# The row of target scores in layer 0: transposed on VectorE in 32x32 blocks before it goes to scratch

## The chip, the cores and the metric

One Trainium2 chip, one core. The time is device microseconds of one execution. Beside the runs that are timed, one execution is taken with the hardware profiler; all rows shown here come from such executions. Engines: PE is TensorE (PEld its weight loads), DVE is VectorE, ACT is ScalarE, POOL is GpSimd, SP is SyncE, which here issues every DMA.

## What is computed

Four graph layers over 32 graphs of 512 nodes with 128 features; every layer is added to its input after a layer norm and a relu. Layers 1 to 3 are products with the adjacency matrix and small weights. The change lies in layer 0, which is a kind of graph attention:

```
x_h   = elu(h @ Wi + bi)                       # h = relu(layernorm(x)), [32, 512, 128]
a_src = x_h @ We[:H, 0]                        # one score per node
a_tgt = x_h @ We[H:, 0]                        # one score per node
e     = sigmoid(a_tgt[:, :, None] + a_src[:, None, :] + be[0])
e     = e * (adj + ALPHA * (1 - (adj != 0)))   # [32, 512, 512]
agg   = einsum('bij,bjh->bih', e, x_h)
self_part = x_h * sum(e, axis=-1)
out   = concat([elu(concat([agg, self_part]) @ Wn + bn), x_h]) @ Wm + bm
```

For e, the target score of every node i is needed along the free axis, on all 128 partitions, while the source score of node j is a value per partition. The scores come out of a matmul with the nodes on the partitions. So the targets have to be turned from columns into a row, and the row spread over the partitions.

## The kernel before

The kernel first lists all operations of all graphs with `op(engine, us, due, emit, reads, writes, ...)`, and then a planner (`Plan.order`) puts them into one fixed order for each engine. The planner keeps a clock of its own: `us` is the time that an operation holds its engine, `result` how much later its output is known, and `due` only ranks the operations that are ready on an engine at a moment. Buffers are slots of a kind: 36 of "f" (SBUF, 128x512), 8 of "s" (SBUF, small), 8 of "b" (PSUM), 4 of "d" (the row, in DRAM), 8 of "m" (DRAM), 6 of "x". An operation that takes a new slot is placed only when one is free on the planner's clock. Operations marked `two`, and all POOL operations, are kept apart in that plan. On the chip the order is fixed, and each instruction waits by semaphores for what it needs, in its engine's order[...]. The plan also exists a second time, for an adjacency matrix that is not exact in a short format; it isn't executed here.

Several graphs are under way at once: while layers 1 to 3 of one group of four graphs run, layer 0 of the next group is woven in between. Layer 1 takes five steps per graph; each ends with `turned` (L333): a transpose in blocks on VectorE (L337), a write to scratch "m" (L340) and a read back in another order (L342), 256 KB each. Then ScalarE rounds the state (L672), VectorE takes the rest (L675), and TensorE multiplies with the adjacency matrix (L686). L352 is the copy of a PSUM result to SBUF; L357 is any product with a 128x128 weight.

Layer 0 of graph b (`layer0`, L455): TensorE forms the messages and the two scores of each node (L469); VectorE scales the scores into the small tile `ends` (L476): columns 0 to 3 are source scores of the four chunks of 128 nodes, columns 4 to 7 the targets. For the first four graphs the targets are spread by TensorE (L493). For the other 28:

```
op("SP", 0.6, due + 10, gather, [ends], [row], result=11.0)
op("SP", 0.6, due + 14, lambda: nc.sync.dma_start(
    at(tgt), at(row).to_broadcast([P, N])), [row], [tgt], keep=KEEP, result=7.0)
```

`gather` (L488) writes the four columns into the 2 KB row "d" in DRAM, one element of 4 bytes at a time, and the read (L502) brings that row to each of the 128 partitions. Then four tanh operations on ScalarE, one for each chunk of source nodes, make e with the source score as bias (L507), VectorE multiplies by the mask (L510), GpSimd adds up (L516), TensorE aggregates (L525).

Of the kernel before, what the change touches and what calls it, by code (L numbers as in the profile page):

```python
# [13 lines left out]
AF = mybir.ActivationFunctionType  # L14
ALU = mybir.AluOpType

P = 128
# [21 lines left out]
class Plan:  # L39
# [13 lines left out]
    def op(self, eng, us, due, emit, reads=(), writes=(), two=False, keep=0, result=None):  # L53

        o = Op(eng, us, self.RESULT[eng] if result is None else result, emit, two, keep)
        for v in reads:
            o.before.add(v.writer)  # L60
        for v in writes:
            o.before.update(v.readers)
            if v.writer:
                o.before.add(v.writer)
            elif v.kind and v.slot is None:
                o.takes.append(v)
        for v in reads:
            v.readers.append(o)
        for v in writes:
            v.writer, v.readers = o, []  # L70
        o.vals = [v.whole or v for v in dict.fromkeys([*reads, *writes])]
        for v in o.vals:
            v.left += 1
        for v in [*reads, *writes, *o.vals]:
            self.vals[v] = True
        o.before -= {o, None}
        o.due = max([due, *(b.due for b in o.before)])
        for b in o.before:
            b.after.append(o)
        self.ops.append(o)  # L80
# [100 lines left out]
def tile_four_graph_layers(  # L181
# [27 lines left out]
    nc = tc.nc  # L209
    B, N, D = x.shape  # L210
    NC = N // P
    G = 4
# [10 lines left out]
    slots = {"x": 6, "f": 36, "q": 4, "s": 8, "d": 4, "m": 8, "b": 8}  # L223
    plan = Plan(slots, ahead=60.0, last=(B - 2) * PACE)
    op = plan.op
# [4 lines left out]
    dram = ctx.enter_context(tc.tile_pool(name="dram", bufs=1, space=bass.MemoryType.DRAM))  # L230

    def buffers(pool, kind, n, shape, dt=F32):
        return [pool.tile(shape, dt, tag=f"{kind}{i}", name=f"{kind}{i}") for i in range(n)]
# [3 lines left out]
        "f": buffers(pool, "f", slots["f"], [P, 512]),  # L237
        "q": buffers(pool, "q", slots["q"], [P, 512], F32R),
        "s": buffers(pool, "s", slots["s"], [P, 12 * NC]),
        "d": buffers(dram, "d", slots["d"], [1, N]),  # L240
        "m": buffers(dram, "m", slots["m"], [P, N]),
        "b": buffers(psum, "b", slots["b"], [P, 512]),
    }
# [1 line left out]
    def at(v):  # L245
        if v.tile is not None:
            return v.tile
        return places[v.kind][v.slot] if v.whole is None else at(v.whole)[:, v.part]
# [8 lines left out]
    def chunks(t):  # L257
        return t.rearrange("p (c d) -> p c d", c=NC)
# [65 lines left out]
    def transposed(src, due):  # L324

        pt = Val("b")
        def emit():
            for c in range(NC):
                nc.tensor.transpose(at(pt)[:, ts(c, P)], at(src)[:, ts(c, P)], at(ident))  # L329
        op("PE", T_TR, due, emit, [src, ident], [pt])  # L330
        return pt
# [18 lines left out]
    def copied(src, due, us=T_COPY):  # L350
        t = Val("f")
        op("ACT", us, due, lambda: nc.scalar.copy(at(t), at(src)), [src], [t])  # L352
        return t
# [58 lines left out]
    for jc in range(NC):  # L412
        pt, z, odd = Val("b"), Val("f"), Val("f")
        def turn(jc=jc, pt=pt):
            for ic in range(NC):
                nc.tensor.transpose(at(pt)[:, ts(ic, P)], at(A_nat[ic])[:, ts(jc, P)], at(ident))
# [38 lines left out]
    def layer0(b, h, due):  # L455
        KEEP = 12
        hT = copied(transposed(h, due), due)
        d = due + 6
        xhT = elu(product(Wi_sb, hT, d), bi_sb, bi_half, d, KEEP)

        d = due + 14
        msg, ends = Val("f"), Val("s")
        for half in range(2):
            pt = Val("b")
            def cut(pt):
                return at(pt)[:, : 2 * (P + 2)].rearrange("p (c d) -> p c d", c=2)
            def send(pt=pt, half=half):
                for c in range(2):
                    nc.tensor.matmul(  # L469
                        cut(pt)[:, c, :], at(xhT)[:, ts(2 * half + c, P)], at(W_tok),  # L470
                        start=True, stop=True,
                    )
            def take(pt=pt, half=half):
                nc.scalar.copy(chunks(at(msg))[:, ts(half, 2), :], cut(pt)[:, :, :P])
            def score(pt=pt, half=half):
                nc.vector.tensor_scalar(  # L476
                    at(ends)[:, : 2 * NC].rearrange("p (k c) -> p c k", k=2)[:, ts(half, 2), :],
                    cut(pt)[:, :, P:], 0.5, at(be_quarter), op0=ALU.mult, op1=ALU.add,
                )
            op("PE", 2 * T_NARROW, d, send, [xhT, W_tok], [pt])  # L480
            op("DVE", 0.14, d, score, [pt, be_quarter], [ends])
            op("ACT", 0.3, d, take, [pt], [msg])

        d = due + 20
        row, tgt = Val("d"), Val("f")
        def gather():
            with nc.allow_non_contiguous_dma(reason="a column of chunks becomes a row"):
                nc.sync.dma_start(  # L488
                    at(row).rearrange("o (c p) -> p (o c)", c=NC), at(ends)[:, NC : 2 * NC]
                )  # L490
        def spread():
            for c in range(NC):
                nc.tensor.transpose(  # L493
                    at(tgt)[:, ts(c, P)],
                    at(ends)[:, NC + c : NC + c + 1].to_broadcast([P, P]), at(ident),
                )
        if b < G:
            tgt = Val("b")
            op("PE", T_TR, d, spread, [ends, ident], [tgt])
        else:  # L500
            op("SP", 0.6, due + 10, gather, [ends], [row], result=11.0)
            op("SP", 0.6, due + 14, lambda: nc.sync.dma_start(  # L502
                at(tgt), at(row).to_broadcast([P, N])), [row], [tgt], keep=KEEP, result=7.0)
        es = []
        for jc in range(NC):
            e = Val("f")
            op("ACT", T_ACT, d, lambda e=e, jc=jc: nc.scalar.activation(  # L507
                at(e), at(tgt), AF.Tanh, bias=at(ends)[:, jc : jc + 1]), [tgt, ends], [e],
                keep=KEEP if jc == 0 else 0)
            op("DVE", T_VEC, d + jc, lambda e=e, jc=jc: nc.vector.scalar_tensor_tensor(  # L510
                at(e), at(e), 1.0, at(mask)[:, jc, :], op0=ALU.add, op1=ALU.mult),
                [e, mask], [e], two=True)
            es.append(e)
        sums = [Val("f"), Val("f")]
        def add(dst, a, c):
            op("POOL", 1.4, d, lambda: nc.gpsimd.tensor_tensor(  # L516
                at(dst), at(a), at(c), op=ALU.add), [a, c], [dst])
        add(sums[0], es[0], es[1])
        add(sums[1], es[2], es[3])
        add(sums[0], sums[0], sums[1])  # L520

        d = due + 30
        pn = Val("b")
        for jc in range(NC):
            op("PE", T_MM, d, lambda jc=jc: nc.tensor.matmul(  # L525
                at(pn), at(msg)[:, ts(jc, P)], at(es[jc]), start=jc == 0, stop=False),
                [msg, es[jc]], [pn])

        if b < G:
            ps = product(ones, sums[0], d)  # L530
        else:
            high, low, ps = Val("q"), Val("q"), Val("b")
            op("ACT", T_COPY, d, lambda: nc.scalar.copy(at(high), at(sums[0])), [sums[0]], [high])
            op("DVE", T_VEC, d, lambda: nc.vector.tensor_tensor(
                at(low), at(sums[0]), at(high).bitcast(F32), op=ALU.subtract),
                [sums[0], high], [low], two=True)
            def total():
                for n, part in enumerate((low, high)):
                    nc.tensor.matmul(at(ps), at(ones_r), at(part), start=n == 0, stop=n == 1)
            op("PE", 2 * T_PASS, d, total, [high, low, ones_r], [ps])  # L540
        own = Val("f")
        op("DVE", T_VEC, d, lambda: nc.vector.tensor_tensor(
            at(own), at(xhT), at(ps), op=ALU.mult), [xhT, ps], [own])
        product(Wn_sb, own, d, pn, start=False)
        recv = elu(pn, bn_sb, bn_half, d + 6, 2, ALPHA / 2)

        d = due + 44
        po = Val("b")
        def emit():
            for c in range(NC):  # L550
                for n, src in enumerate((recv, xhT)):
                    nc.tensor.matmul(  # L552
                        at(po)[:, ts(c, P)], at(src)[:, ts(c, P)], at(Wm_sb)[:, n, :],
                        start=n == 0, stop=n == 1,
                    )
        op("PE", 8 * T_NARROW, d, emit, [recv, xhT, Wm_sb], [po])
        add_to_x(b, po, d)
# [294 lines left out]
```

## Time and profile before

| | before |
|---|---|
| median of 3 runs | 1746.38 us (1745.01 to 1746.55) |
| profiled execution, its own time | 1748.12 us |
| its span in the profile | 1746.3 us |
| PE busy | 1695.5 us, 97% |
| DVE busy | 1479.3 us, 85% |
| ACT busy | 1135.2 us, 65% |
| POOL busy | 399.8 us, 23% |
| moved by DMA | 112.07 MB, mean 64 GB/s |

A row of the table of groups names the line, the engine, the operation and the tiles (out<-in, with buffer numbers left out), then the shapes, how often it ran, its busy time in us and the mean ns of one, and behind the second bar the idle time of the engine just before these instructions with what ended it. In a timeline, each row has its start in us, its duration, and in brackets the idle time of the engine before it and the releaser. In the list of DMA issues the last number is the median time in us from issue to landing. In a list of waits the three numbers are the us in total, how often, and the longest. PE's ends are modelled, so its busy time is somewhat too large.

### The profile page before, as it was taken

The page shows a single profiled execution, that of the slowest core. Times are in us where ns is not written, and L with a number is a line of the kernel's source. Part 1 is how long each engine was busy: PE and PEld are TensorE (multiplying, and loading weights), DVE is VectorE, ACT ScalarE, POOL GpSimd, SP SyncE. Part 2 cuts the span into 40 slices and gives each one's busy share as a digit, 9 for nine tenths or more (in the row PEclk, how much of TensorE's full clock was granted, in tenths as well). Part 3 has the DMA queues.
Part 4 walks back from the last instruction along what each step waited for, and adds up shares of the span by engine and source line. Part 5 has one row for each costly group of instructions (what it writes and reads, how often), then busy time and mean ns, then how long its engine had stood idle before and what let it go on. Part 6 is the DMA issues. An engine that isn't in the chain of part 4 may idle for free.

```text
span 1746.3 us, 21006 instructions
## 1 busy us (share of the span) xinstructions
PE 1695.5 (97%) x6829; PEld 1098.0 (63%) x6829; DVE 1479.3 (85%) x3213; ACT 1135.2 (65%) x2155; POOL 399.8 (23%) x312
## 2 busy tenths in 40 slices
PE   5899999999999999999999999999999999999998
PEld 3555555566666666665666666666666656656797
DVE  6899999999898887888888898888899879878752
ACT  6767765778666666665765667666768656655451
POOL 4521210332222211222212221122232212001110
PEclk9999999999999999999999999999999999999999
DMA  4022322322222222223221221222322131221201
GB/s 109 7 53 75 85 73 73 81 52 85 52 58 61 79 67 46 74 75 55 67 55 60 79 61 61 67 52 81 67 67 55 50 84 61 73 72 58 76 13 48
DMA packets 164534, 112.07 MB, mean 64 GB/s; under 512 B 23232, under 2 KB 139840, under 8 KB 164416
## 3 DMA queue, kind: packets, MB, share of 16 engines
q1 hardware_dynamic: 164416, 110.65, 23.9%
q8 instruction: 55, 0.90, 0.3%
q14 instruction: 63, 0.52, 0.2%
HBM read 60.23 MB, written 50.39 MB: 63 GB/s over the span
## 4 chain that ended last, share of the span: by engine, by line
PE 76%; DVE 13%; DMA 4%; ACT 3%; issue 2%; SPq 0%; DVEq 0%; ACTq 0%
PE b L357 33%; PE b L686 17%; PE b L769 9%; PE b L760 6%; DMA f<-m 4%; PE b L525 4%; PE b L552 3%; DVE f L510 2%; PE b L329 2%; DVE f L704 2%; PE b L743 2%; PE b L469 1%; DVE f L337 1%; DVE f L723 1%; DVE r L675 1%
## 5 line engine op out<-in xcount | busy, mean ns | idle before, releaser
L686 PE MATMUL b<-A_r,r 128*128 128x512 f32 x1536 | 427.6, 421 | 4.3 <-DVE r L675 4.2
L352 ACT COPY f<-b 128x512 f32<-128x512 f32 x448 | 256.5, 588 | 210.6 <-PE b L686 119.2
L686 PEld LDWEIGHTS b<-A_r,r 128*128 128x128 f32 x1536 | 287.2, 189 | 109.6 <-issue 38.9
L391 POOL TENSOR_TENSOR s<-s,nhalf 128x4 f32<-128x4 f32 x128 | 156.2, 1221 | 735.9 <-DVE s L389 707.8
L769 PE MATMUL b<-r,A_r 128*128 128x512 f32 x768 | 306.3, 499 | 0.0
L704 DVE TENSOR_TENSOR f<-f,b 128x512 f32<-128x512 f32 x320 | 213.6, 679 | 56.5 <-PE b L357 54.0
L399 ACT ACTIVATE f<-x,s 128x128 f32<-128x128 f32 x512 | 209.9, 488 | 22.3 <-DVE s L394 22.2
L769 PEld LDWEIGHTS b<-r,A_r 128*128 128x128 f32 x768 | 140.6, 189 | 102.6 <-issue 91.5
L516 POOL TENSOR_TENSOR f<-f,f 128x512 f32<-128x512 f32 x96 | 154.1, 1608 | 207.4 <-DVE f L510 131.1
L362 ACT ACTIVATE f<-f,b4w 128x512 f32<-128x512 f32 x160 | 115.8, 724 | 127.3 <-DVE f L704 126.6
L337 DVE STREAM_TRANSPOSE f<-f 128x512 f32<-128x512 f32 x160 | 176.5, 1105 | 0.3
L675 DVE TENSOR_TENSOR r<-f,r 128x512 fp32r<-128x512 f32 x192 | 141.3, 739 | 37.1 <-ACT r L672 37.0
L357 PE MATMUL b<-f,u5T 128*128 128x512 f32 x320 | 163.2, 595 | 8.7 <-DVE f L711 8.7
L357 PE MATMUL b<-f,w4T 128*128 128x512 f32 x320 | 165.2, 599 | 4.1 <-ACT f L352 4.0
L357 PE MATMUL b<-f,w3T 128*128 128x512 f32 x320 | 163.8, 594 | 0.0
L357 PE MATMUL b<-f,w5T 128*128 128x512 f32 x320 | 163.2, 595 | 0.0
L357 PE MATMUL b<-f,u3T 128*128 128x512 f32 x320 | 162.7, 592 | 0.0
L721 DVE TENSOR_TENSOR f<-f,f 128x512 f32<-128x512 f32 x160 | 121.5, 761 | 39.3 <-ACT f L362 39.1
L760 PEld LDWEIGHTS b<-V,f 128*128 128x128 f32 x1024 | 131.7, 191 | 31.1 <-issue 25.1
L362 ACT ACTIVATE f<-b,b5w 128x512 f32<-128x512 f32 x160 | 109.7, 688 | 60.4 <-PE b L357 60.2
L362 ACT ACTIVATE f<-f,b3w 128x512 f32<-128x512 f32 x160 | 115.0, 721 | 50.8 <-DVE f L704 50.5
L525 PE MATMUL b<-f,f 128*128 128x512 f32 x256 | 130.9, 596 | 3.2 <-issue 3.0
(95 smaller groups left out, 2489.9 us busy)
## 6 DMA issues: line engine op xcount, KB each, us to landing
m<-f SPq DMA_DIRECT2D x160, 256.0 KB, 2.0
f<-m SPq DMA_DIRECT2D x160, 256.0 KB, 2.8
x<-in_x_dram SPq DMA_DIRECT2D x32, 256.0 KB, 4.5
out_dram<-x SPq DMA_DIRECT2D x32, 256.0 KB, 2.4
f<-d SPq DMA_DIRECT2D x28, 256.0 KB, 4.1
f<-in_adj_dram SPq DMA_DIRECT2D x4, 256.0 KB, 4.6
f<-in_L_gnn_weight_dram SPq DMA_DIRECT2D x2, 224.0 KB, 2.6
d<-s SPq DMA_DIRECT2D x28, 2.0 KB, 9.1
```

The lines of the kernel that those rows point to most:

```text
L337: op("DVE", 1.03, due, lambda: nc.vector.transpose(at(blocks).rearrange("p (q c f) -> p q c f", c=NC, f=32), at(src).rearrange("p (c i q) ...
L352: op("ACT", us, due, lambda: nc.scalar.copy(at(t), at(src)), [src], [t])
L357: op("PE", T_MM, due, lambda: nc.tensor.matmul(at(dst), at(w), at(src), start=start, stop=stop), [src, w], [dst])
L362: op("ACT", us, due, lambda: nc.scalar.activation(at(dst), at(src), AF.Tanh, bias=at(bias), scale=scale), [src, bias], [dst])
L391: op("POOL", 1.2, due, lambda: nc.gpsimd.tensor_tensor(stat(SCALE), stat(VAR), at(neg_half), op=ALU.pow), [s, neg_half], [s])
L399: nc.scalar.activation(at(h)[:, ts(c, P)], at(X[b])[:, c, :], AF.Relu, bias=stat(SHIFT)[:, c : c + 1], scale=stat(SCALE)[:, c : c + 1],)
L525: op("PE", T_MM, d, lambda jc=jc: nc.tensor.matmul(at(pn), at(msg)[:, ts(jc, P)], at(es[jc]), start=jc == 0, stop=False), [msg, es[jc]], [pn])
L675: op("DVE", T_VEC, due, lambda: nc.vector.tensor_tensor(part(lo), whole(), part(hi).bitcast(F32), op=ALU.subtract), [src, hi], [lo], two=two)
L686: nc.tensor.matmul(at(pa), at(part)[:, ts(jc, P)], at(adjT)[:, jc, :], start=jc == n == 0, stop=jc == NC - 1 and n == PARTS - 1,)
L704: op("DVE", T_VEC, d, lambda: nc.vector.tensor_tensor(at(s), at(u), at(pg), op=ALU.add), [u, pg], [s])
L760: nc.tensor.matmul(at(pz)[:, ts(i, D)], at(hT[i])[:, ts(ic, P)], at(V[k]), start=i == 0, stop=last and i == G - 1,)
L769: nc.tensor.matmul(at(pz), at(adjT)[:, jc, ts(ic, P)], at(part), start=False, stop=jc == NC - 1 and n == PARTS - 1,)
```

## The change

The four columns of target scores are first repeated eight times along the free axis, to 32 columns, and transposed on VectorE inside blocks of 32x32, into a new small tile `flip`. Then row 32q + 4k + c of `flip` holds the targets of chunk c on the partitions 32q to 32q + 31, for each k from 0 to 7. The whole tile, 128 rows of 32 values (128 bytes), goes to a scratch buffer "d" of that shape. The read takes the first four rows of each quarter, 512 bytes that lie together, four such pieces for each partition. So the row is then ordered by (quarter, chunk, place), and the tanh reads it in runs of 32 elements and writes its output in the plain order. The planner is given other numbers: the gather and the read have due time d = due + 20 instead of due + 10 and due + 14, and smaller `us` and `result`. Only the graphs from 4 on are concerned; for the first four, the branch with TensorE stays.

```
-        "d": buffers(dram, "d", slots["d"], [1, N]),
+        "d": buffers(dram, "d", slots["d"], [P, 32]),
...
         row, tgt = Val("d"), Val("f")
+
+        flip = Val("s")
+        def turn():
+            nc.vector.transpose(
+                at(flip)[:, :32].rearrange("p (k c) -> p k c", c=NC),
+                at(ends)[:, None, NC : 2 * NC].to_broadcast([P, 32 // NC, NC]))
         def gather():
-            with nc.allow_non_contiguous_dma(reason="a column of chunks becomes a row"):
-                nc.sync.dma_start(
-                    at(row).rearrange("o (c p) -> p (o c)", c=NC), at(ends)[:, NC : 2 * NC]
-                )
+            nc.sync.dma_start(at(row), at(flip)[:, :32])
+        def read():
+            rows = at(row).rearrange("(q k) i -> q (k i)", k=32)[:, :P]
+            nc.sync.dma_start(
+                at(tgt).rearrange("p (q e) -> p q e", e=P), rows[None].to_broadcast([P, 4, P]))
+        def of_tgt():
+            if b < G:
+                return at(tgt)
+            return at(tgt).rearrange("p (q c i) -> p c q i", c=NC, i=32)
+        def like_tgt(t):
+            return t if b < G else t.rearrange("p (c q i) -> p c q i", c=NC, i=32)
...
-            op("SP", 0.6, due + 10, gather, [ends], [row], result=11.0)
-            op("SP", 0.6, due + 14, lambda: nc.sync.dma_start(
-                at(tgt), at(row).to_broadcast([P, N])), [row], [tgt], keep=KEEP, result=7.0)
+            op("DVE", 0.1, d, turn, [ends], [flip])
+            op("SP", 0.5, d, gather, [flip], [row], result=2.6)
+            op("SP", 0.5, d, read, [row], [tgt], keep=KEEP, result=3.6)
...
             op("ACT", T_ACT, d, lambda e=e, jc=jc: nc.scalar.activation(
-                at(e), at(tgt), AF.Tanh, bias=at(ends)[:, jc : jc + 1]), [tgt, ends], [e],
+                like_tgt(at(e)), of_tgt(), AF.Tanh, bias=at(ends)[:, jc : jc + 1]), [tgt, ends], [e],
                 keep=KEEP if jc == 0 else 0)
```

## The prediction

> **What bounds the kernel now.** I read the busy table first, then the chain that ended last with its pieces in order of time, then the timeline around the longest pieces.
>
> ```profile
> span 1746.3 us, 21006 instructions
> PE 1695.5 (97%) x6829; PEld 1098.0 (63%) x6829; DVE 1479.3 (85%) x3213; ACT 1135.2 (65%) x2155; POOL 399.8 (23%) x312
> ...
> PE 76%; DVE 13%; DMA 4%; ACT 3%; issue 2%; SPq 0%; DVEq 0%; ACTq 0%
> ```
>
> TensorE is the bound: 97% busy, and the change takes no matmul away. So only PE's idle time can be won. PE's busy time in the first 60 us counts as full, but I went through the start times of its matmuls one after the other and took every interval that is over 0.44 us longer than the usual one of its kind: these add to 46 us, 19 us of them before 71 us (loads, the branch, the first graphs, which don't use the changed path). Some 27 us are left, spread over 21 places. That is the most that this change could win, about 1.5%.
>
> The chain has one non-compute item that doesn't belong there, 4% on DMA. Its pieces over 5 us, from the chain in order of time:
>
> ```profile
> 304.07 11.68 DMA f<-m
> ...
> 355.81 11.54 DMA f<-m
> ...
> 518.30 11.87 DMA f<-m
> ...
> 687.14 11.45 DMA f<-m
> ...
> 793.07 11.55 DMA f<-m
> ...
> 1417.19 12.21 DMA f<-m
> ```
>
> These six are reads of layer 1's turned state (L342). The page's list of DMA issues says what such a read takes normally:
>
> ```profile
> m<-f SPq DMA_DIRECT2D x160, 256.0 KB, 2.0
> f<-m SPq DMA_DIRECT2D x160, 256.0 KB, 2.8
> ...
> f<-d SPq DMA_DIRECT2D x28, 256.0 KB, 4.1
> ...
> d<-s SPq DMA_DIRECT2D x28, 2.0 KB, 9.1
> ```
>
> The smallest transfer is the slowest: d<-s, the gather that the change replaces, 2 KB in 9.1 us. SP's own timeline shows it just ahead of a stalled read:
>
> ```profile
> 303.59 0.37 SPq L488 DMA_DIRECT2D d<-s  x1
> 304.07 0.45 SPq L342 DMA_DIRECT2D f<-m  x1
> 304.56 0.51 SPq L290 DMA_DIRECT2D x<-in_x_dram  x1
> ```
>
> and the whole core's timeline shows the end of that stall:
>
> ```profile
> 315.77 0.62 ACT L672 CAST r<-f 128x512 fp32r<-128x512 f32 x1 [3.53 <-DMA f<-m]
> ...
> 316.42 0.69 DVE L675 TENSOR_TENSOR r<-f,r 128x512 fp32r<-128x512 f32 x1 [3.53 <-ACT r L672]
> ...
> 317.17 2.99 PE L686 MATMUL b<-A_r,r 128*128 128x512 f32 x8 [2.11 <-DVE r L675]
> ```
>
> The read lands 11.7 us after issue instead of 2.8; ACT waits 3.53 us for it, then VectorE, then PE idles 2.11 us. In the same view PE idles behind the others by 0 (after 367 us), 0.76 (533.5), 1.44 (699.8), 2.15 (806.4) and 1.81 us (1430.6). The sum is 8.3 us. The other 22 gathers delay transfers too, but PE has other work then.
>
> [...] the gather is 4-byte packets, most of the page's 23232 under 512 B. [...] The trace shows the 4-byte case alone. [...] L711, usually 0.68 us, takes 1.75 beside the adds of L516, at a place where PE waits:
>
> ```profile
> 929.53 1.75 DVE L711 SCALAR_TENSOR_TENSOR f<-f,f 128x512 f32<-128x512 f32 x1
> ...
> 931.34 1.12 PE L357 MATMUL b<-f,u5T 128*128 128x512 f32 x2 [2.08 <-DVE f L711]
> ```
>
> Five such places (825.0, 874.6, 931.3, 1038.1, 1333.7 us) idle PE by 1.79, 0.86, 2.08, 1.01 and 1.42, together 7.2 us. The change doesn't touch these adds.
>
> **The change part by part.** All of it concerns graphs 4 to 31: 28 of each.
>
> *Gather.* 512 pieces of 4 bytes become 128 pieces of 128. No row shows that transfer. Lower bound: m<-f, also 128 rows from SBUF to scratch, 2.0 us. Upper bound: if the excess of the old gather (9.1 - 2.0 = 7.1) goes with the number of pieces, 2.0 + 7.1 x 128/512 = 3.8. I take 2.5. The bytes rise from 2 to 16 KB, against 256 KB of m<-f. Then the six reads land after about 2.8 to 4 us, ahead of ACT: **-8.3 us**. The neighbour x load is shorter too, but nothing on the chain waits for it. Of stalls that PE doesn't feel I count nothing.
>
> *The VectorE transpose.* 28 of 128x32. L337 takes 1.10 us for 512 columns; the small operations L389 and L394 take 0.19 to 0.20. I take 0.2: 5.6 us on an engine that is idle for 267. It stands right after the second score on the same engine and its source is that score, so it waits for no new engine; a few wait also for an old DMA to leave the s buffer. Its cover is the matmuls of the other graphs under way. VectorE is on 13% of the chain, so 13% of 5.6, **+0.7 us**; bounds 0 and 5.6.
>
> *Read.* 128 pieces of 2 KB become 512 of 512 bytes, the shape of f<-m (2.8 us) but out of one 2 KB set for all partitions, as the old read (4.1 us, up to 5.8). Bounds 2.8 and 5.8, I take 4.0.
>
> *Tanh.* L507 now reads 32-element runs. L672 reads such runs in most of its r<-f group: 624 ns mean, against 586 for r<-b. At most 0.04 x 112 = 4.5 us on ACT, which is idle 611: nothing; without that cover, up to +4.5.
>
> *Order and queue.* The planner charged the old path 0.6 + 11 + 0.6 + 7 = 19.2 us. It charges the new one 0.6 + 3.1 + 4.1 = 7.8. In the trace the tanh of the graph scored at 303.6 starts at 326.7, and the L507 group had no idle time at all before it: never was a target late. Now the tanh is put some 11 us earlier; f buffers (xhT, msg) come free earlier by as much; an s buffer is taken in addition. SP's place for the read moves to at most 4 issues behind the gather (before up to 7). While it waits there, the L340 and L342 issues queue behind it, and ACT through them; that was
>
> ```profile
> SPq L502 <- DMA d<-s: 31.0, 8, 7.6
> ```
>
> and falls with the landing, to under 2 us each. My path is 0.2 + 2.5 + 4.0 and some 0.2 for hand-overs, 6.9 us against the 7.8 planned, so the tanh waits for nothing. The new order on every engine [...] of either sign, and I give it 0, with +-6 us.
>
> Sum: -8.3 + 0.7 = -7.6. The profiled execution took 1748.1 us, 1.8 outside its span, and was 1.7 above the median of 1746.4. I expect a span of 1738.7, and a median of 1746.4 - 7.6 = **1738.8**.
>
> **The rivals.** *Targets too late (slower).* The earlier tanh stands in ACT's fixed order with little margin. With both upper bounds the path is 0.2 + 3.8 + 5.8 + 0.2 = 10.0, 2.2 later than planned. From the stalls: ACT idle of 3.53, 3.30, 3.66 and 3.62 us cost PE 2.11, 1.44, 2.15 and 1.81, so about 1.4 to 1.9 us are absorbed. Being 2.2 late costs PE 0.3 to 0.8 per graph, at 0.7 some 20 us over 28 graphs, less the 8.3 won: 1746.4 + 11 = 1757. It decides from a lateness of about 1.4 + 8.3/28 = 1.7 us. Against it: my middle values leave 0.9 us to spare; for it: the old plan's margin was about 6 us, and nothing was late.
>
> *Already covered (same).* The next late thing takes over: where a read now comes in time, [...] the new order brings as many collisions as it removes stalls: 1745. For it: collisions idle PE nearly as long (7.2 us) as the stalls do, and the plan's prices don't see them drift. Against it: after the stalls ACT, VectorE and PE all stand still, so nothing else was late there.
>
> *Pieces of 128 bytes are as slow as those of 4.* The stalls stay and the tanh comes 5.5 us late: 28 x about 4 = 112 us slower. Against it: nothing in the old transfer but its piece count is large. 2 in 100.
>
> **How the numbers follow.** A measurement here tells 0.2%, 3.5 us, from no change. The main case is 64 in 100, with its own range of 1730 to 1743 (8.3 plus the collisions' 7.2 gone at best; half the gain lost at worst). Covered: 18. Late targets or an unlucky order: 16, slow pieces 2. Faster 0.65, same 0.18, slower 0.17. The range of 1729 to 1755 leaves out the worst of the late targets and a gain beyond 17 us.
>
> **What would show it.** d<-s landing near 2.5 us; no f<-m piece of 11 us in the chain and L672's wait for f<-m (23.0 us) under 5; the L507 group without idle time; VectorE up by 5 to 6 us; PE's busy time unchanged. It is wrong if ACT idles before L507 behind f<-d by over 1.5 us a graph, if d<-s still takes over 5 us, or if the 11 us pieces go and the span stays: then the gaps stand behind VectorE.

## The result, and the profile after

The median is 1730.3 us (1729.2 to 1731.05) against 1746.5 before: 16.2 us less, a ratio of 0.9908 with a 95% interval of 0.9891 to 0.9925. The forecast was 7.6 us less. The direction and the mechanism were right, but the gain is twice what the sum gave. So terms of the sum were too small, and the experiments look for them.

The page of the kernel after, with the lines that answer to those shown of before (span, busy time, chain by engine, DMA issues with the us to landing last):

```profile
span 1729.2 us, 21107 instructions
...
PE 1690.5 (98%) x6829; PEld 1097.8 (63%) x6829; DVE 1476.3 (85%) x3241; ACT 1138.0 (66%) x2155; POOL 398.9 (23%) x312
...
PE 89%; DVE 7%; ACT 2%; issue 1%; DMA 0%; SPq 0%; DVEq 0%; ACTq 0%
...
m<-f SPq DMA_DIRECT2D x160, 256.0 KB, 2.0
f<-m SPq DMA_DIRECT2D x160, 256.0 KB, 2.9
...
f<-d SPq DMA_DIRECT2D x28, 256.0 KB, 4.9
...
d<-s SPq DMA_DIRECT2D x28, 16.0 KB, 1.4
```

The gather carries eight times the bytes and lands in 1.4 us instead of 9.1. DMA is gone from the chain (4% before): no f<-m piece of 11 us is left in it. The groups by shape show the new transpose and the tanh:

```profile
L520 ACT ACTIVATE f<-f,s 128x512 f32<-128x512 f32 x112 | 72.7, 715 | 2.2 <-DMA f<-d 2.2
...
L489 DVE STREAM_TRANSPOSE s<-s 128x32 f32<-128x32 f32 x28 | 5.7, 205 | 0.1
```

The tanh in runs of 32 elements takes 715 ns as before, and in all 28 graphs it waits for its target once, for 2.2 us. The transpose takes 205 ns.

What PE does between 75 and 1640 us, behind the first graphs and ahead of the tail, can be read from the busy times of that stretch, first of before, then of after (after the stretch's length: PE busy, number of matmul records in it, and so on for PEld, DVE, ACT and POOL; then the clock, DMA share, GB/s):

```profile
75.00:1640.00 1565.00, 1543.02 (x5996) 977.69 (x5995) 1372.39 (x2914) 1044.71 (x1970) 346.50 (x253) 1.00 0.25 66
```

```profile
75.00:1640.00 1565.00, 1552.46 (x6108) 989.74 (x6107) 1386.80 (x2985) 1061.09 (x1997) 349.25 (x259) 1.00 0.22 67
```

PE idles 1565.0 - 1543.0 = 22.0 us before and 12.5 us after. That is 9.5 us, near the forecast. Over the whole of the two spans, which differ by 17.1 us, PE's idle time fell by 12.1 us (50.8 to 38.7). The other 5.0 us are time in which PE was busy and got less done, for the matmul records are the same 6829. The trace of before has four places in this stretch where that can be seen; this is the same view, cut to them:

```profile
318.20:321.40 3.20, 3.20 (x7) 1.97 (x6) 3.20 (x6) 1.93 (x4) 0.00 (x0) 0.50 0.62 179
806.40:809.50 3.10, 3.10 (x4) 1.49 (x5) 1.89 (x4) 3.10 (x8) 0.59 (x1) 0.50 0.30 91
932.60:935.80 3.20, 3.20 (x7) 1.98 (x6) 3.20 (x6) 1.21 (x2) 0.00 (x0) 0.50 0.06 24
1431.00:1434.20 3.20, 3.20 (x12) 2.32 (x11) 2.77 (x4) 0.74 (x2) 0.00 (x0) 0.50 0.30 85
```

In each, the granted TensorE clock (the share of full speed at which TensorE was allowed to run) is 0.50. They stand right behind the four longest idle times of PE in that stretch: 2.11 us at 317.2, 2.15 at 806.4 and 1.81 at 1430.6, all three behind a stalled read, and 2.08 at 931.3, a collision: L711 took 1.75 us there instead of its usual 0.68, beside GpSimd's adds of L516. For the collisions that the prediction counts, the trace shows the overlap in time and no cause: two other L711 that ran wholly inside the time of such an add, at 94.7 and 1249.8 us, took 0.70 and 0.69. The clock's own records give each of the four stretches 3.41 us. At half speed that is 0.5 x 3.41 = 1.7 us of work lost each, 6.8 us together. The trace of after has none of them in this stretch, but more half speed at its start. The first 75 us, of before and then of after:

```profile
0.00:75.00 75.00, 51.64 (x227) 32.56 (x228) 56.40 (x163) 51.86 (x107) 39.74 (x47) 0.95 0.24 64
```

```profile
0.00:75.00 75.00, 53.92 (x217) 34.05 (x218) 53.88 (x156) 49.94 (x103) 39.38 (x46) 0.89 0.23 64
```

So the 5.0 us of busy time are a balance of both. Such counts hold for one execution each: in another trace of the same kernel (the run of after beside the two other plans, below) the first 75 us have a clock of 0.93, and there is a stretch of half clock at 420.8 us.

### The profile page after: what moved, and what is told of

Its sections match the earlier page's. It is cut to its first block, busy times and chain, and to the rows that moved or that the text cites. A ratio compares the mean times of both kernels' runs of the same rounds, so it can differ in the third digit from the quotient of the medians.

```text
span 1729.2 us, 21107 instructions
## 1 busy us (share of the span) xinstructions
PE 1690.5 (98%) x6829; PEld 1097.8 (63%) x6829; DVE 1476.3 (85%) x3241; ACT 1138.0 (66%) x2155; POOL 398.9 (23%) x312
## 4 chain that ended last, share of the span: by engine, by line
PE 89%; DVE 7%; ACT 2%; issue 1%; DMA 0%; SPq 0%; DVEq 0%; ACTq 0%
PE b L357 39%; PE b L699 19%; PE b L782 10%; PE b L773 6%; PE b L538 5%; PE b L565 3%; PE b L329 2%; DVE f L523 2%; PE b L469 2%; PE b L756 1%; DVE r L688 1%; PE b L552 1%; DVE f L717 1%; ACT f L399 1%; DVE f L724 1%
## 5 line engine op out<-in xcount | busy, mean ns | idle before, releaser
L699 PE MATMUL b<-A_r,r 128*128 128x512 f32 x1536 | 421.5, 417 | 5.6 <-DVE r L688 5.4
L782 PE MATMUL b<-r,A_r 128*128 128x512 f32 x768 | 309.8, 503 | 0.0
```

The costliest lines, as they stand in the source:

```text
L699: nc.tensor.matmul(at(pa), at(part)[:, ts(jc, P)], at(adjT)[:, jc, :], start=jc == n == 0, stop=jc == NC - 1 and n == PARTS - 1,)
L782: nc.tensor.matmul(at(pz), at(adjT)[:, jc, ts(ic, P)], at(part), start=False, stop=jc == NC - 1 and n == PARTS - 1,)
```

## The experiments

Theory A says: the gain lies in the transfers; a stalled read costs its idle time, and in addition a halved clock behind a long one. Its rivals: each stall costs its idle time alone and the new order gave the rest (B), the order gave everything (C), the clock has nothing to do with idle time (D), the old gather hurt only through the target's own path (E).

The medians of before differ between the sessions: 1760.5 us in the first (runs e1, e2, e4), 1745.9 in both others. Ratios are taken within a session.

**New transfers in the old order.** Every engine's order is that of before; only the transpose is added, inside the second score operation.

```
             def score(pt=pt, half=half):
                 nc.vector.tensor_scalar(...)
+                if half and b >= G:
+                    nc.vector.transpose(
+                        at(ends)[:, 16:48].rearrange("p (k c) -> p k c", c=NC),
+                        at(ends)[:, None, NC : 2 * NC].to_broadcast([P, 32 // NC, NC]))
...
+            nc.sync.dma_start(at(row), at(ends)[:, 16:48])
...      # read, of_tgt, like_tgt and "d" as in the change; due and result as before
```

> The kernel before with the new transfers alone: the 32x32 transpose sits inside the second score operation and writes into spare columns of the same small tile, the gather writes 128 pieces of 128 bytes, the read takes 512 pieces of 512 bytes, the tanh reads the new order. The planner keeps the old numbers (11 and 7 us), so every engine has the order of before. Theory A (transfers; each stall costs its idle time and a halved TensorE clock after it): the five stalls, 14.6 us of PE time lost in the trace of before, go: 1732 us (1729 to 1736), no read f<-m over 6 us in the chain, and the three stretches of clock 0.5 behind them gone; the losses beside GpSimd's adds stay. Rival B (stalls cost their idle time of 8.3 us and no more, the rest came from the new order): 1738 us. Rival C (all from the new order): 1746 us.

Measured: 1732.3 us, ratio 0.9847 (0.9833 to 0.986) to a before of 1760.5. No f<-m read is left in the chain, PE idles 12.6 us between 75 and 1640, and no half clock lies there. The time is A's. But with a before that was 14 us slower than usual, the size of the gain says little; so it was run again, beside the kernel after.

**The kernel after and the new transfers alone, side by side.**

> The kernel after, unchanged, beside the new transfers in the old order on one chip. Theory A (all of the gain lies in the transfers): the two agree within 4 us; by the traces the new order loses 3.5 us more than the old one before 300 us and 1 to 2 us less later, so after is 0 to 3 us slower. Rival B (the new order gives a part of its own): after is 5 us faster or more.

> The new transfers in the old order once more, on the same chip as the kernel after: theory A expects a ratio to before between 0.985 and 0.992, and within 0.003 of that of the kernel after; rival B 0.995.

Measured: after 1730.4 us, 0.9913 (0.9900 to 0.9926); the new transfers alone 1734.3 us, 0.993 (0.9917 to 0.9943). So 11.6 us of the 15.5 come with the transfers alone; B's 1738 is too slow and C's 1746 is out. But after is the faster one by 3.9 us, where A expected it to be 0 to 3 us slower. The new order seems to give a part. It is less than rival B's 5 us, and the intervals of the two ratios overlap, so its size is rough. The traces differ at one place, for example: in the old order the collision near 920 us (1.75 us of VectorE) still idles PE for 2.07 us; in the new one, as long, it idles PE for 0.61. VectorE's and PE's rows of the new transfers alone:

```profile
919.91 1.75 DVE L721 SCALAR_TENSOR_TENSOR f<-f,f 128x512 f32<-128x512 f32 x1
```

```profile
921.72 1.12 PE L357 MATMUL b<-f,u5T 128*128 128x512 f32 x2 [2.07 <-DVE f L721]
```

and of after (L724 is the same operation):

```profile
915.58 1.75 DVE L724 SCALAR_TENSOR_TENSOR f<-f,f 128x512 f32<-128x512 f32 x1
...
917.39 1.12 PE L357 MATMUL b<-f,u5T 128*128 128x512 f32 x2 [0.61 <-DVE f L724]
```

But the new order has idle times of its own, 1.60 us at 380.1 and 1.85 us at 423.0. Between 75 and 1640 us PE idles 12.6 and 14.1 us in the two traces of the new transfers alone, and 12.5 and 12.6 us in two of after. So where the 3.9 us come from is not shown.

**The old transfers in the new order.**

```
+            with nc.allow_non_contiguous_dma(...):
+                nc.sync.dma_start(
+                    at(row).rearrange("o (c p) -> p (o c)", c=NC), at(ends)[:, NC : 2 * NC])
-            nc.sync.dma_start(at(row), at(flip)[:, :32])
...      # "d" as [1, N], read and tanh as before; the transpose is still done
```

> The kernel after with the old transfers: 512 pieces of 4 bytes, one 2 KB row read by each partition, tanh in plain order; the VectorE transpose is still done and its result not used. The order on every engine is that of after, which has the tanh 7.8 us behind the scores by plan. Theory A: the target comes about 0.2 + 9.1 + 4.1 + waits = 14 us behind the scores, some 6 us late, in each of 28 graphs; PE idles 4 to 5 us each, with the halved clock behind it 6: 1746 + 28 x 4 to 6 = 1860 to 1915 us, and ACT idles before the tanh behind f<-d. Rival C (the order alone makes the gain): 1735 us or less.

Measured: 1867.9 us, ratio 1.0611 (1.0595 to 1.0628). The order alone is no gain; made for a target after 7.8 us, it needs one. ACT's list of waits:

```profile
ACT f L521 <- DMA f<-d: 136.4, 28, 9.3
```

28 waits of 4.9 us on average. Twenty stretches of half clock follow between 75 and 1640 us, and the mean clock fell to 0.967. That is the forecast's slower rival, at a lateness well beyond the point where it decides.

**An idle gather added.** This separates what the gather does to others from what it does to its own target: the new transfers in the old order, and behind each gather one of the old kind into a row that nobody reads.

```
             nc.sync.dma_start(at(row), at(ends)[:, 16:48])
+            with nc.allow_non_contiguous_dma(...):
+                nc.sync.dma_start(
+                    places["w"][b % 4].rearrange("o (c p) -> p (o c)", c=NC), at(ends)[:, NC : 2 * NC])
```

> The new transfers in the old order, and right behind each new gather an old one as well: 512 pieces of 4 bytes into a 2 KB scratch row that nobody reads. The target's path doesn't wait for it; one SP issue more for 28 graphs. Theory A (the slow gather hurts by holding up other transfers): landing of 9 us or more, five or so reads f<-m of 11 us again in the chain, idle time of PE behind them as before, and the time of before: ratio 0.996 to 1.002. Rival E (the old gather hurt only through the target's own path): ratio as without it, 0.985 to 0.990.

Measured: 1759.0 us, ratio 1.0078 (1.0063 to 1.0094), 25 us above the same kernel without it and more than A's 0.996 to 1.002. SP's timeline and the core's around one stall (line numbers are shifted):

```profile
311.20 0.43 SPq L494 DMA_DIRECT2D w<-s  x1
311.73 0.44 SPq L343 DMA_DIRECT2D f<-m  x1
```

```profile
323.62 0.62 ACT L687 CAST r<-f 128x512 fp32r<-128x512 f32 x1 [4.39 <-DMA f<-m]
...
325.02 1.38 PE L701 MATMUL b<-A_r,r 128*128 128x512 f32 x4 [2.98 <-DVE r L690]
```

It is the same place and the same chain as at 317 us in before, with PE idle for 2.98 us instead of 2.11. Eight f<-m reads of 11.5 to 12.0 us are back in the chain, four stretches of half clock stand between 75 and 1640 us, and PE idles 1565.0 - 1535.4 = 29.6 us there. At the five places where PE idled 8.3 us in before it idles 11.6 us here. So the old gather needs nothing of its own target to hold up PE, and rival E is out. The idle gather lands in 9.4 us (list of DMA issues):

```profile
d<-s SPq DMA_DIRECT2D x28, 16.0 KB, 1.4
w<-s SPq DMA_DIRECT2D x28, 2.0 KB, 9.4
```

One more stall of this run is the target's own. By the chain a target's read, issued behind the idle gather at 84.7 us, takes 13.8 us, and a stretch of half clock follows this row:

```profile
98.54 2.56 ACT L522 ACTIVATE f<-f,s 128x512 f32<-128x512 f32 x4 [6.25 <-DMA f<-d]
...
100.04 1.56 PE L540 MATMUL b<-f,f 128*128 128x512 f32 x2 [3.77 <-DVE f L525]
```

That is 3.8 + 1.7 = 5.5 of the 25 us, and a part of why the run is slower than before. In all of this the held-up reads were issued on the same queue as the gather; whether a read on another queue would be held up as well was not tried.

**The same, with its pieces 64 bytes apart.** Is it their number, or where they lie in scratch? A landing of 2 to 4 us would speak for their places.

```
-        places["w"][b % 4].rearrange("o (c p) -> p (o c)", c=NC), ...       # [1, N]
+        places["w"][b % 4][:, :, 0][:, :, None], ...                        # [P, NC, 16]
```

> As the run with the idle gather added, but the 512 pieces of 4 bytes of the added gather land 64 bytes apart in a scratch area of 32 KB[...]. If the number of pieces makes the gather slow and holds up the rest: landing over 7 us, reads f<-m of 10 us or more in the chain, ratio to before about 1.00 to 1.01. [...] landing of 2 to 4 us, no such reads, ratio 0.985 to 0.995.

```profile
d<-s SPq DMA_DIRECT2D x28, 16.0 KB, 1.4
w<-s SPq DMA_DIRECT2D x28, 2.0 KB, 2.8
```

Measured: 1735.8 us, ratio 0.9933 (0.9912 to 0.9954), as without any added gather, and no slow read in the chain. So 512 pieces of 4 bytes land in 2.8 us when they lie apart, and in 9.4 when 16 of them lie side by side in 64 bytes. With the number of pieces unchanged, their places in scratch decide. This run changes the distance of the pieces and with it which partitions' pieces are neighbours; the two were not separated, and at which distance the slow landing ends was not tried.

**Pieces of 16 bytes, no transpose.**

```
+            nc.sync.dma_start(at(row), at(ends)[:, NC : 2 * NC])            # "d" is [P, NC]
+            nc.sync.dma_start(at(tgt), at(row).rearrange("p c -> (p c)")[None].to_broadcast([P, N]))
...
+            return at(tgt) if b < G else at(tgt).rearrange("p (i c) -> p c i", c=NC)   # of_tgt
```

> The kernel before with another gather: the four target columns go out as they lie, 128 pieces of 16 bytes into 2 KB of scratch in (place, chunk) order; the read brings this row to every partition as before, 128 pieces of 2 KB; the tanh reads every fourth element. No transpose on VectorE; order of before on every engine. If the number of pieces makes the gather slow: it lands within 1.4 to 2.5 us and the time is that of the new transfers in the old order, about 1732 us. If the smallness of a piece[...] makes it slow: landing over 5 us, stalls left, 1740 us or more. The tanh with a stride of 16 bytes: 712 ns as before, or more (at 2 x 712 it adds 80 us to ACT and shows in the time).

Measured: the gather lands in 1.5 us, and the time is 1749.3 us, ratio 0.9938 (0.9923 to 0.9954), against 0.9847 of the 128-byte pieces in the same session. No slow f<-m read is in the chain. The tanh is the likely reason that the gain is smaller:

```profile
L509 ACT ACTIVATE f<-f,s 128x512 f32<-128x512 f32 x112 | 128.8, 1225 | 0.0
```

1225 ns instead of 715, 57 us more on ScalarE. That is what the VectorE transpose is for: it brings runs of 32 elements, and the tanh takes 715 ns on those as it did before.

**Idle time and the clock, by themselves.** Bursts of matmuls with idle times between, and nothing else. In the first version only the first matmul of a burst depended on the copies, and the others were placed ahead of them, so that no idle time arose. Theory A's 1.8 us and 3.4 us in the expectation are an estimate, which fits what the trace of before shows: behind PE's 1.44 us at 699.8 the clock stayed at 1.00, and behind the 1.81 us at 1430.6 it was 0.50 for 3.41 us.

> Not the layers: the outputs are filled with zeros, and TensorE alone runs, six groups of ten bursts of 16 matmuls (128x512 f32, about 13.7 us a burst), with idle times ahead of the bursts that ScalarE copies make: one to five copies in a chain (0.6 us each, and a third group with a short third copy), so about 0.8, 1.4, 1.7, 2.0, 2.6 and 3.2 us. Theory A: behind an idle time of under about 1.8 us the granted clock stays at 1; behind a longer one it is 0.5 for 3.4 us, so a burst takes 1.7 us more: groups 1 and 2 have clock 1.00, groups 5 and 6 about 1 - 0.5 x 3.4 / 17 = 0.90. Rival D (the 0.5 stretches have nothing to do with idle time): no difference between the groups.

The clock stayed at 1.00 throughout, and this decided nothing. In the second, all matmuls of a burst read the last copy's output:

```
-            nc.tensor.matmul(pt[i % 4], w, a, start=True, stop=True)
+            nc.tensor.matmul(pt[i % 4], w, first, start=True, stop=True)
```

> Not the layers: outputs filled with zeros; six groups of ten bursts of 16 matmuls (128x512 f32, 13.7 us a burst), each burst held back by a chain of ScalarE copies of the burst before: one, two, two and a short one, three, four, five copies, so idle times of about 0.9, 1.5, 1.8, 2.1, 2.7 and 3.3 us. Every matmul of a burst reads the last copy's output, so none can go ahead. Theory A: groups 1 and 2 keep the granted clock at 1.0; the longer the idle time the more bursts start with 3.4 us at 0.5: some in groups 3 and 4, all in group 6, 1.7 us lost each. Rival D (the clock is independent of idle time): no difference between the groups.

The busy times of the six groups, with the granted clock behind POOL's columns:

```profile
35.00:183.00 148.00, 140.75 (x323) 60.28 (x322) 0.00 (x0) 5.86 (x10) 0.00 (x0) 1.00 0.00 0
183.00:337.00 154.00, 140.20 (x322) 60.05 (x321) 0.00 (x0) 12.03 (x20) 0.00 (x0) 1.00 0.00 0
337.00:493.00 156.00, 138.72 (x318) 59.30 (x316) 0.00 (x0) 14.95 (x30) 0.00 (x0) 1.00 0.00 0
493.00:663.00 170.00, 149.60 (x322) 63.51 (x323) 0.00 (x0) 18.26 (x31) 0.00 (x0) 0.95 0.00 0
664.00:838.00 174.00, 147.22 (x320) 62.77 (x319) 0.00 (x0) 24.37 (x40) 0.00 (x0) 0.95 0.00 0
838.00:1033.00 195.00, 161.43 (x321) 67.93 (x320) 0.00 (x0) 30.55 (x50) 0.00 (x0) 0.88 0.00 0
```

By the start times of the matmuls the idle times of the groups are 0.9, 1.5, 1.9, 2.2, 2.8 and 3.5 us. The first three groups never lose the clock (1.00 in these rows). In the fourth (0.95), 6 of 10 bursts start with it halved, in the fifth (0.95) 4, in the sixth (0.88) all. Rival D is out. In the trace of before, the four stretches of half clock start at 318.12, 806.23, 932.52 and 1430.87 us by the clock's records, 143, 37 and 146 times 3.413 us apart; whether such a step decides which bursts are hit, and so why 4 and 6 of 10 are, was not shown. Here 2.2 us was enough in some bursts, and in the kernel before it was 1.97 by the same measure (1.81 in the timeline's bracket, which starts from the modelled end).

The length of one idle time does not decide alone in the kernels either. The kernel after idles as long at one place in two traces, and only in the second (the run beside the two other plans) is the clock halved behind it, so that the eight matmuls take longer:

```profile
423.04 2.11 PE L699 MATMUL b<-A_r,r 128*128 128x512 f32 x8 [1.85 <-DVE r L688]
```

```profile
420.62 3.63 PE L699 MATMUL b<-A_r,r 128*128 128x512 f32 x8 [1.85 <-DVE r L688]
```

In the run v3 below, the clock is halved from 337.8 us on behind two shorter idle times:

```profile
336.09 0.74 PE L549 MATMUL b<-q,ones_r 128*128 128x512 f32 x2 [1.08 <-DVE q L544]
337.30 3.39 PE L696 MATMUL b<-A_r,r 128*128 128x512 f32 x8 [0.47 <-DVE r L685]
```

And in the second trace of the new transfers alone it is not halved behind 2.17 us (at 815.5) and 2.07 us (at 921.7, the row shown above).

**Two other plans for the new transfers.** The planner was told what the trace of after shows (v1: gather 0.5 + 1.3, read 0.5 + 4.9), or the transpose was put inside the score operation, without a buffer of its own, and the read was charged more (v3: 0.5 + 2.6 and 0.5 + 5.2). After was run beside them.

```
-            op("SP", 0.5, d, gather, [flip], [row], result=2.6)
-            op("SP", 0.5, d, read, [row], [tgt], keep=KEEP, result=3.6)
+            op("SP", 0.5, d, gather, [flip], [row], result=1.3)                  # v1
+            op("SP", 0.5, d, read, [row], [tgt], keep=KEEP, result=4.9)
+            op("SP", 0.5, d, gather, [ends], [row], result=2.6)                  # v3
+            op("SP", 0.5, d, read, [row], [tgt], keep=KEEP, result=5.2)
```

> The kernel after, but the planner is told what the trace of after shows: gather 0.5 + 1.3, read 0.5 + 4.9 in place of 0.5 + 2.6 and 0.5 + 3.6. The sum to the target is the same 7.8 us; only the place of the read on SP moves up. Theory A: nothing of the transfers changes, so within 4 us of the kernel after; the order differs in places [...].

> The kernel after with the transpose inside the second score operation, its result in spare columns of the same small tile (no s buffer more, no VectorE operation of its own to be placed), and a planner told 0.5 + 2.6 and 0.5 + 5.2. Theory A: within 4 us of the kernel after, either side; only if the s buffer or the separate transpose cost anything is it faster by more.

> The kernel after on the same chip, for the comparison with the two variants: ratio to before 0.985 to 0.993.

Measured: v1 1724.8 us, 0.988 (0.9862 to 0.9898); v3 1721.2 us, **0.9853** (0.9836 to 0.9871); after 1730.7 us, 0.9912 (0.989 to 0.9935). Both are more than 4 us below after, against the expectation, and v3 beats both kernels. The stretch of 75 to 1640 us of v1 and of v3:

```profile
75.00:1640.00 1565.00, 1557.78 (x6161) 997.44 (x6160) 1391.24 (x3008) 1060.94 (x2001) 352.34 (x260) 1.00 0.22 67
```

```profile
75.00:1640.00 1565.00, 1562.06 (x6174) 1000.10 (x6173) 1387.22 (x3017) 1062.35 (x2005) 363.12 (x261) 1.00 0.22 67
```

PE idles 7.2 and 2.9 us, where after idles 12.5. v1 moves no transfer's shape and only shifts the plan's numbers, so the order by itself is worth 6 us here. Which of v3's two edits gave its further 4 us was not separated.

## Why the prediction was right and where it was wrong

*The cause.* Right: the old gather held up reads of layer 1 (six of 11.5 to 12.2 us in the chain of before, where 2.8 is the median), and the added idle gather shows that it does so without any part in the target's own path (eight of 11.5 to 12.0). All five stalls that idled PE are gone.

*The two terms that failed.* The sum gave -8.3 + 0.7 = -7.6 us for the transfers and 0 for the order. Side by side, the transfers alone gained 11.6 us and the order another 3.9: the first term was too small by 4.0, the second by 3.9, and together that is 15.5 instead of 7.6.

*The term -8.3 us.* It priced a stall at PE's idle time, from the brackets of the timeline. In the profiled execution of before, three of the five stalls were followed by half clock, which took 3 x 1.7 = 5.1 us more. The evidence was in that trace. A matmul record at 806.4 us lasted 1.22 us where its like lasts 0.59, and in the row shown for 317.17 eight matmuls take 2.99 us where eight of their like took 2.40 at 302.2; I took these rows' brackets and didn't read their durations. The collision at 931.3 was followed by half clock as well, but in the two traces of the new transfers alone the same collision, idling PE for as long, was not.

How much of the 4.0 us the halved clock explains in the medians is open. From the mean clock of each execution and its span, I estimate (1 minus the mean clock, times the span) that 11.3 us were lost to half speed in an average execution of before in that session, 9.5 with the new transfers alone and 10.7 in after. That is 1.8 and 0.6 us less, not 5.1 or 6.8. These means also hold the start-up, where executions of one kernel differ (0.93 and 0.89 in the first 75 us of two traces of after). So that a stall can cost more than its idle time is shown; that it is the whole of the 4.0 us is not.

*The VectorE transpose, +0.7.* 5.7 us in all, as forecast; no wait at it is seen. Its net cost was not measured by itself.

*Gather and read.* I took 2.5 and 4.0 us; they landed in 1.4, below my lower bound, and in 4.9. The upper bound of the gather went with the number of pieces, and the spread pieces, 512 of them in 2.8 us, show that this scaling was not the reason. The sum, 6.3 against 6.5, was right, and so was the conclusion: one tanh waits, 2.2 us. SP's wait for the gather fell from 31.0 us to this, again under 2 us each:

```profile
SPq L496 <- DMA d<-s: 18.6, 19, 1.7
```

*Tanh.* No cost at 32 elements, as said: 715 ns before and after. The price of 0.04 us at most was too high here, and the run with 16-byte steps, at 1225 ns, shows that such a cost is real elsewhere.

*The signs.* The landing and the chain came out as listed, and ScalarE's 23.0 us of waits for f<-m are gone. Two signs did not come out. VectorE's busy time fell by 3.0 us, where I expected 5 to 6 more. In the two traces of the new transfers in the old order it rose from 1479.3 to 1482.2 and 1485.3, so it is the new order that shortens it. PE's fell by 5.0, where I expected no change; with the work unchanged, that is the balance of half clock again.

*Order: 0, with +-6.* The order was worth some 3.9 us of gain beside the new transfers, within these bounds but not nothing. That it came out as a gain is luck of this plan: the sum had no reason for a sign, and two other plans, one of them with the transpose moved as well, gave 6 and 9 us more.

*Open.* The first session's before of 1760.5 us is not explained, and the third session, on the same chip, had 1745.9: no trace of the slower one was taken, and its mean clock of 0.990 to 0.993 only says that more of it ran at half speed than in the 0.992 to 0.996 of the other sessions.

## What to carry to other kernels

A stall of the bounding engine is not priced by its idle time alone: look at the clock behind it, and read the durations of the matmuls there. Here an idle time of TensorE of about 2 us could cost 1.7 us more, but not every one did, so a price from one trace is the price of one execution. A transfer can be tiny and still hold up others, as the 2 KB in 9.1 us did here with reads of 11.5 to 12.2 us behind it; the us from issue to landing, set beside its bytes, finds it, and a copy of it that nobody reads shows what it does. A planner's prices can be worth as much as an edit: one shift of two numbers gave 6 us here. Whether prices nearer to what is measured give the better order was not shown.

## What the runs showed of the hardware that I had not expected

512 pieces of 4 bytes, written to scratch side by side, landed in 9.1 us (before) and 9.4 (the idle gather); the same pieces 64 bytes apart landed in 2.8 us, 128 pieces of 16 bytes in 1.5, and 128 pieces of 128 bytes in 1.4. These 1.4 us are less than the 2.0 us of 256 KB in 128 rows; a transfer of the same bytes in larger pieces was not run, so what the size of a piece costs there is not shown. ScalarE read runs of 32 f32 elements as fast as a plain row (715 ns for 128x512), but single elements 16 bytes apart took 1225 ns. TensorE's clock was halved for 3.41 us behind each of four idle times of 1.81 to 2.15 us in one trace of before, in one run behind 1.08 and 0.47 us; in another it stayed whole behind 2.17 and 2.07 us.
